# A graph-attention layer on one core: value products ahead of their softmax, and a tail with its own order

## The chip, the cores and the metric

The kernel runs on one core of one Trainium2 chip. The metric is device time in microseconds (us) of one execution. Three executions of the kernel before took 4083.7, 4086.26 and 4088.33 us; the median, 4086.26 us, is the time before.

## What is computed

A graph has 12500 nodes with 128 features each, and 400000 edges that are sorted by their target node. Each node's row goes through a layer norm and a ReLU to give h. Then, cut to what matters:

```
message = (h @ w_src + b_src)[src] + (h @ w_dst)[dst]
message = message * edge_weight * radial_mlp(edge_attr_32)
msg     = (message @ w_sep + b_sep).reshape(E, 8, 32)
alpha, value = smooth_leaky_relu(msg[:, :, :16]), msg[:, :, 16:]
score   = einsum('ehk,ahk->eh', alpha, alpha_dot)
att     = segment_softmax(score, dst)           # over the edges of a target
out     = segment_sum(value * att, dst) @ w_proj + b_proj
return x + out
```

So per edge there is a gathered row, a small perceptron of the edge's attributes, eight scores and a value row of 128; per target node there is a softmax over its edges and a weighted sum of values, which is projected and added to x.

## The kernel before

**Pairs, steps and lag.** Edges are cut into sections of 512 (four tiles of 128), and two sections make a pair; there are NP = 391 pairs, the last one short. A *half* is one section (c, f) of pair c. The loop calls `step(k)` for k = -5 to 390 and works on several pairs at once, in an order that is written out by hand: in step k it gathers the rows of pair k + 2, makes the message mT of pair k, the alphas of pair k - 1, and, for the pair c = k - LAG = k - 12, the weighted values and, one step later, the sums. The lag is there because the softmax runs over groups of MP = 8 pairs: eight pairs' scores are collected, then `softmax_up`, `softmax_down`, `softmax_sub` and `softmax_exp` scan them on DVE and ACT, and `softmax_T` turns the result into Pem, the attention factors by edge. Group 48, the last, has seven pairs, 384 to 390.

**The engines in a step.** POOL gathers each section by four indirect DMAs (L1018). PE turns the gathered rows and adds the targets' rows (L1078, L1090), multiplies for the perceptron (L1034, L1047, L1062), for the alphas (pa, L1101), the scores (L1118), the values (V, L1233) and the sums (L1246). V is one PSUM bank: `values(c, f)` multiplies mT of the half by w_v into it, and DVE multiplies V by Pem into pvx (L1235). `sums` multiplies pvx by a one-hot matrix oh of 64 targets (L1217, L1220) and DVE moves the sum with an addition to a tile ob (L1250). DVE also makes rad, mT and al (L1067, L1095, L1108), ACT the activations (sl is L1103). An engine takes its instructions in the order written, so an instruction that waits holds up those behind it.

**Where the sums go.** SP stores ob to two tables: whole windows of 64 targets to win (`store_win`), and rows of targets that lie inside one section to agg (`store`, two a pair, each after a value load of the row's place). Targets whose edges cross a section's end are combined from win later: `block_rows`, `block_columns`, `block_totals`, `block_quotients` and `rows_end`, for 13 blocks of 128 section ends; the last two blocks, 11 and 12, belong to the tail. Their rows are written to out by `scatter` (POOL, L1445).

**Units.** A unit is 512 rows of agg. `load_unit` and `load_x` bring its sums (gu) and its rows of x (xs); two steps later it has been divided by the softmax sums, turned, multiplied by w_proj, added to x and stored to out (L1303, L1308, L1312 to L1320, L1326, L1334, L1340, L1341). UNIT_STEP lists the steps at which the 23 units begin: before, the last ones are 366, 376, 386, 390 and 394.

**Direct pairs.** The last DIRECT = 13 pairs, 378 to 390, end too late for agg. For them `direct_quotients` divides the sums at once (L1264 to L1267), `direct_turn` and `direct_out` turn and project them and add the rows of x (L1272 to L1280), and `direct_scatter` writes them to out by target (POOL, L1287). Every such scatter and those of the blocks come after the last unit's store to out in the order of writes.

**The tail before.** After the loop POOL gathers 13 times rows of x by target for the direct pairs (L1460), loads the finished block rows, adds the output bias to the x rows (L1648) and gathers 13 times x for the blocks (L1454). Then `step(k)` is called 13 times more, for k = 391 to 403, with other conditions in it for k >= NP, and a list `jobs` puts the last blocks between the steps. The twelve pairs 379 to 390 get their V, their one-hots and their sums there. `sum_rows` (POOL, L1658) adds x to the block rows.

Of the kernel before, what the change touches and what calls it, by code (L numbers as in the profile page):

```python
# [55 lines left out]
def gnn_kernel(ctx: ExitStack, tc: tile.TileContext, a: dict, out: bass.AP):  # L56
# [19 lines left out]
    xb = dram.tile([N, C], F32, name="xb")  # L76
    win = dram.tile([NS * W, ROW], F32, name="win")
# [19 lines left out]
    assert D < IN_AGG and done(UNIT_STEP[-1]) < NS and UNITS * UNIT + P * 4 >= N - UNIT  # L97
    NF = N // P
# [82 lines left out]
    with tc.tile_pool(name="node", bufs=2) as np_, tc.tile_pool(name="node1", bufs=1) as n1, \  # L181
# [223 lines left out]
        def fits():  # L405
# [35 lines left out]
            nc.sync.dma_start(out=t_dst[N:N + W, :], in_=bare[:W, 0:C])  # L441
            nc.sync.dma_start(out=eb.rearrange("p s i -> p (s i)"),
# [470 lines left out]
    def windows():  # L913
# [7 lines left out]
        with tc.tile_pool(name="ps", bufs=1, space=PSUM) as pp, \  # L921
# [176 lines left out]
            def alphas(k, f):  # L1098
                pa = pp.tile([C, SEC], F32, name="pa")
# [124 lines left out]

            def values(c, f):
                if c >= NP - LAG and f == 0:
                    V = pms[:, c % 2, :].rearrange("p (t c) -> p t c", c=C)
                else:
                    V = pv
                n = tiles(c, f)  # L1230
                for t in range(n):
                    o = f * SEC + t * T
                    nc.tensor.matmul(V[:, t, :], mTs[c][:, o:o + T], w_v, start=True, stop=True)  # L1233
# [26 lines left out]

            def direct_quotients(c):
                o = accs[c]
                rd = sp.tile([P, H], F32, name="dr")
                nc.vector.tensor_scalar(rd, o[:, C:ROW], 1e-16, None, op0=ALU.add)  # L1264
# [3 lines left out]
                                     o[:, 0:C].rearrange("p (h k) -> p h k", h=H),  # L1268
                                     rd.unsqueeze(2).to_broadcast([P, H, C // H]))

            def direct_turn(c):
                nc.tensor.transpose(p3[:, 0, 0:P], dqs.pop(c), ident)  # L1272
                qTs[c] = sp.tile([P, C], F32, name="dT")
                nc.scalar.copy(qTs[c], p3[:, 0, 0:P])

            def direct_out(c):
                py = p3[:, 1, 0:C]
# [27 lines left out]
            def load_x(u, pool):  # L1305
                n0, n1, n = unit_rows(u)
                xs[u] = pool.tile([P, 4, C], F32, name="xs", bufs=1)
                (nc.scalar if u == UNITS - 1 else nc.sync).dma_start(out=xs[u][:n], in_=x[n0:n1, :].rearrange("(p t) c -> p t c", t=4))  # L1308
# [150 lines left out]
            def rows_dx(c):  # L1459
                nc.gpsimd.indirect_dma_start(  # L1460
                    out=xw_at(c), out_offset=None, in_=x[:, :],
                    in_offset=bass.IndirectOffsetOnAxis(ap=ids_d[:, c - D:c - D + 1], axis=0),
                    bounds_check=N - 1, oob_is_err=False)
# [25 lines left out]

            def step(k):  # L1490
                c = k - LAG
                if has(c - 2) and k <= NP:
# [16 lines left out]
                if has(c - 2) and k <= NP and c - 2 < IN_AGG:  # L1509
# [5 lines left out]
                if k % 16 == 7 and has(k + 9):  # L1515
                    prep_make((k + 9) // 16)
                unit = k >= UNIT_STEP[0]
# [10 lines left out]
                if k >= NP:  # L1528
                    m, r = LAST_M + 1, k - NP
                if has(c):  # L1530
                    weights(c)
                    values(c, 0)
# [8 lines left out]
                if c - 2 >= D and has(c - 2):  # L1541
                    direct_turn(c - 2)
# [11 lines left out]
                if has(k):  # L1554
                    mlp3(k)
                if has(k + 1):
# [6 lines left out]
                if has(c - 1):  # L1563
                    sums(c - 1)
                    if k >= NP:
                        if k == NP + LAG:
                            last_rows_2()
                        else:
                            store_win(c - 1)
# [279 lines left out]
```

## Time and profile before

| | before |
|---|---|
| time, median of 3 executions | 4086.26 us |
| the profiled execution's own time | 4089.07 us |
| its span, first to last instruction | 4087.2 us |
| PE busy | 3865.2 us (95%) |
| DVE busy | 3104.5 us (76%) |
| POOL busy | 3065.6 us (75%) |
| ACT busy | 1862.3 us (46%) |
| granted TensorE clock, mean | 0.985 |

The profiled execution is one more than the three, and a little longer than their median. Times within it count from the span's start. "Busy" leaves out what an engine spends on issuing, so an engine that issues DMAs back to back is not at 100%. In the rows of groups, the columns are line, engine, operation, output <- inputs with shapes, count, then busy us, mean ns of one, and the idle time ahead of them with what ended it; in rows of the timeline, the first two numbers are start and duration in us.

### The profile page before, as it was taken

The page shows a single profiled execution, that of the slowest core. Times are in us where ns is not written, and L with a number is a line of the kernel's source. Part 1 is how long each engine was busy: PE and PEld are TensorE (multiplying, and loading weights), DVE is VectorE, ACT ScalarE, POOL GpSimd, SP SyncE. Part 2 cuts the span into 40 slices and gives each one's busy share as a digit, 9 for nine tenths or more (in the row PEclk, how much of TensorE's full clock was granted, in tenths as well). Part 3 has the DMA queues.
Part 4 walks back from the last instruction along what each step waited for, and adds up shares of the span by engine and source line. Part 5 has one row for each costly group of instructions (what it writes and reads, how often), then busy time and mean ns, then how long its engine had stood idle before and what let it go on. Part 6 is the DMA issues. An engine that isn't in the chain of part 4 may idle for free.

```text
span 4087.2 us, 84249 instructions
## 1 busy us (share of the span) xinstructions
PE 3865.2 (95%) x27811; PEld 2349.3 (57%) x27811; DVE 3104.5 (76%) x5557; ACT 1862.3 (46%) x3782; POOL 3065.6 (75%) x3244
## 2 busy tenths in 40 slices
PE   7899999999999999999999999999999999999997
PEld 6356555655555555555555555555555556556555
DVE  6677777777777777777777777777777777777777
ACT  5454444444444444444444444444444444444451
POOL 6777777777777777777777777777777777777775
PEclk9999999999999999999999999999999999999998
DMA  7777777677767777777777777777777777777772
GB/s 242 214 186 194 182 193 193 184 182 190 191 169 195 186 191 172 196 187 180 185 192 185 190 189 197 194 174 192 197 194 183 185 191 198 182 195 193 186 177 55
DMA packets 536579, 762.21 MB, mean 186 GB/s; under 512 B 126743, under 2 KB 339769, under 8 KB 536006
## 3 DMA queue, kind: packets, MB, share of 16 engines
q1 hardware_dynamic: 378142, 498.27, 41.8%
q0 software_dynamic: 101872, 207.34, 24.5%
q10 hardware_dynamic: 56120, 51.10, 4.5%
q8 instruction: 226, 3.70, 0.4%
q14 instruction: 219, 1.79, 0.2%
HBM read 632.27 MB, written 125.70 MB: 185 GB/s over the span
## 4 chain that ended last, share of the span: by engine, by line
PE 68%; DMA 12%; POOL 7%; issue 5%; DVE 5%; ACT 2%; SPq 1%; ACTq 0%; DVEq 0%; POOLq 0%
PE V L1233 15%; PE pa L1101 14%; DMA gs<-t_src,idx 8%; PE misc L1246 8%; PE pm L1078 7%; PE p L1062 6%; POOL gs L1018 6%; PE m L1034 5%; PE pm L1090 4%; PE p L1047 4%; PE m L1118 3%; DMA agg<-ob 1%; DVE mT L1095 1%; POOL mT L1018 1%; DMA win<-ob 1%
## 5 line engine op out<-in xcount | busy, mean ns | idle before, releaser
L1018 POOL DMA_INDIRECT gs<-t_src,idx x3021 | 2875.4, 952 | 923.0 <-issue 768.5
L1103 ACT ACTIVATE sl<-pa,c_b_a 128x512 f32<-128x512 f32 x782 | 537.6, 687 | 1089.2 <-PE pa L1101 1085.1
L1108 DVE SCALAR_TENSOR_TENSOR al<-pa,sl 128x512 f32<-128x512 f32 x782 | 536.8, 686 | 527.6 <-ACT sl L1103 520.5
L1233 PEld LDWEIGHTS V<-c_w_v,mT 128*128 128x128 f32 x6154 | 753.3, 193 | 309.9 <-DVE ob L1250 119.9
L1233 PE MATMUL V<-c_w_v,mT 128*128 128x128 f32 x6154 | 886.3, 287 | 8.1 <-DVE pvx L1235 8.1
L1101 PE MATMUL pa<-mT,c_w_a 128*128 128x512 f32 x1564 | 839.2, 619 | 26.6 <-DVE mT L1095 23.5
L1235 DVE TENSOR_TENSOR pvx<-V,Pem 128x512 f32<-128x512 f32 x770 | 528.4, 686 | 207.9 <-PE V L1233 191.1
L1049 ACT ACTIVATE h<-p,b 128x512 f32<-128x512 f32 x391 | 469.2, 1200 | 427.5 <-PE p L1047 328.4
L1078 PEld LDWEIGHTS pm<-ident,gs 128*128 128x128 f32 x3021 | 375.2, 141 | 481.9 <-issue 463.8
L1067 DVE SCALAR_TENSOR_TENSOR rad<-p,c_fc_b,w_b 128x1024 f32<-128x1024 f32 x391 | 500.5, 1280 | 105.6 <-PE p L1062 87.3
L1246 PEld LDWEIGHTS misc<-pvx,oh 128*64 128x64 f32 x6250 | 353.1, 138 | 295.0 <-ACT h L1037 284.5
L1078 PE MATMUL pm<-ident,gs 128*128 128x128 f32 x3021 | 458.6, 275 | 64.5 <-DMA gs<-t_src,idx 64.4
L1095 DVE SCALAR_TENSOR_TENSOR mT<-pm,c_b_src,rad 128x1024 f32<-128x1024 f32 x391 | 497.6, 1273 | 7.7 <-PE pm L1090 7.2
L1246 PE MATMUL misc<-pvx,oh 128*64 128x136 f32 x6250 | 453.2, 287 | 0.9 <-ACT h L1037 0.3
L1062 PE MATMUL p<-h,w3b 64*128 64x512 f32 x1564 | 405.9, 596 | 0.5 <-ACT h L1049 0.4
L1034 PE MATMUL m<-eT,w1b 64*128 64x256 f32 x782 | 276.7, 434 | 20.3 <-ACT qT L1328 15.1
L1090 PE MATMUL pm<-ohT,m 64*128 64x512 f32 x1564 | 287.3, 445 | 0.0
L1101 PEld LDWEIGHTS pa<-mT,c_w_a 128*128 128x128 f32 x1564 | 237.3, 192 | 76.8 <-DVE mT L1095 44.5
L1034 PE MATMUL misc<-eT,w1b 64*128 64x256 f32 x782 | 276.8, 434 | 0.0
L1037 ACT ACTIVATE h<-misc,b 128x256 f32<-128x256 f32 x391 | 185.4, 474 | 193.9 <-PE misc L1034 181.1
L1134 ACT ACTIVATE Sp<-m,b_s 128x512 f32<-128x512 f32 x192 | 131.8, 686 | 308.5 <-PE m L1118 302.0
L1217 DVE TENSOR_TENSOR oh<-lane,misc 128x504 f32<-128x504 f32 x391 | 261.2, 668 | 0.1
(216 smaller groups left out, 3550.8 us busy)
## 6 DMA issues: line engine op xcount, KB each, us to landing
w_b<-in_edge_weight SPq DMA_DIRECT2D x390, 512.0 KB
d_b<-in_dst SPq DMA_DIRECT2D x390, 256.0 KB
e_t<-in_edge_attr ACTq DMA_DIRECT2D x386, 128.0 KB
sc_d<-Sp SPq DMA_DIRECT2D x192, 256.0 KB
gs<-t_src,idx POOLq DMA_INDIRECT x3021
win<-ob SPq DMA_DIRECT2D x390, 68.0 KB
agg<-ob SPq DMA_DIRECT2D x762, 33.5 KB
md<-t_dst SPq DMA_DIRECT2D x782, 32.0 KB
```

What stands on the lines that cost most here:

```text
L1018: sent = [nc.gpsimd.indirect_dma_start(out=gs[:, t, :], out_offset=None, in_=t_src[:, :], in_offset=bass.IndirectOffsetOnAxis(ap=idx[:, t0 ...
L1034: nc.tensor.matmul(p1[f], w1b[s, :], eTs[k][s, :], start=True, stop=True)
L1062: nc.tensor.matmul(p3[:, f, 0:SEC], w3b[s, :], h2s[k][s, :], start=True, stop=True)
L1067: nc.vector.scalar_tensor_tensor(rad[:, 0:n], p3.rearrange("c f e -> c (f e)")[:, 0:n], b3, w_g[k][:, 0:n], op0=ALU.add, op1=ALU.mult)
L1078: turned = [nc.tensor.matmul(pm[:, t * T:(t + 1) * T], gs[:, t, :], ident, start=(t == 0), stop=False, is_transpose=True, skip_group_check ...
L1095: nc.vector.scalar_tensor_tensor(mTs[k][:, 0:n], pms.rearrange("c f e -> c (f e)")[:, 0:n], b_n, rad[:, 0:n], op0=ALU.add, op1=ALU.mult)
L1101: nc.tensor.matmul(pa[:, 0:n], w_a, mTs[k][:, f * SEC:f * SEC + n], start=True, stop=True)
L1103: nc.scalar.activation(sl[:, 0:n], pa[:, 0:n], AF.Silu, bias=b_a, scale=1.0)
L1108: nc.vector.scalar_tensor_tensor(al, pa, 0.25, sl, op0=ALU.mult, op1=ALU.add)
L1233: nc.tensor.matmul(V[:, t, :], mTs[c][:, o:o + T], w_v, start=True, stop=True)
L1235: nc.vector.tensor_mul(pvx[c][:, f, 0:n, 0:C].rearrange("p t (h k) -> p t h k", h=H), V[:, 0:n, :].rearrange("p t (h k) -> p t h k", h=H), ...
L1246: nc.tensor.matmul(acc[f * W:(f + 1) * W, :], ohs[c][:, f * TS + t, :], pvx[c][:, f, t, :], start=(t == 0), stop=(t == n - 1), skip_group_ ...
```

## The change

It has four parts.

1. **Value products ahead.** `values` is split. `product_v` makes V; `values_ahead` does that for a half whose softmax may not be there yet, and ACT copies V back over the half's own mT. `values` then multiplies by Pem from that copy. `plan(k)` hands out the halves in order, two a step as before and three at steps 311, 315, ... 387, at three spots of the step. After the loop four halves are left: those of pairs 389 and 390.
2. **Units.** The late units begin at 376, 381, 387 and 393 in place of 376, 386, 390 and 394: one more is done within the loop.
3. **Rows of x.** A table xp in memory holds the last 2048 rows of x with the output bias added; it is made in steps 40 to 47 (`padded_rows`). SP loads each direct pair's two windows of 64 consecutive rows from it, in the last three steps of the loop and one in the tail (`rows_dx`). POOL's 13 gathers and its additions go. The last unit's x comes from xp as well.
4. **A tail of its own.** The extra 13 calls of `step` are replaced by a list written out, with `slot(c)` as its repeated part. The sums of a direct pair start from a product of the identity with the matrix bare, stay in PSUM for the quotients, and are copied to ob by ACT; they stand ahead of the turning of an older pair. The rows of x are added by PE (identity times the rows, into the same sum) and ACT copies the result. The softmax of group 48 stands ahead of the slots 380 to 390. The block rows come back by SP, and so do the last rows of block 12 (`last_rows_2`).

The diff, cut to its core:

```diff
-UNIT_RUNS = ((96, 32, 4), (204, 13, 7), (296, 10, 10), (390, 4, 2))
+UNIT_RUNS = ((96, 32, 4), (204, 13, 7), (296, 10, 9), (381, 6, 3))
+EXTRA = 311
...
+            def values_ahead(c, f, V):
+                n = tiles(c, f)
+                product_v(c, f, V)
+                nc.scalar.copy(value_slot(c, f)[:, 0:n, :], V[:, 0:n, :])
+                ahead.add((c, f))
...
             def values(c, f):
+                n = tiles(c, f)
+                if (c, f) in ahead:
+                    V = value_slot(c, f)
                 else:
                     V = pv
+                    product_v(c, f, V)
...
+            def direct_start(c):
+                accs[c] = half[:, 0:ROW] if c == D else pms[:, c % 2, 0:ROW]
+                nc.tensor.matmul(accs[c], ident, bare, start=True, stop=False, skip_group_check=True)
+            def direct_sums(c):
+                acc = accs[c]
...
+                            nc.tensor.matmul(acc[f * W:(f + 1) * W, :], ohs[c][:, f * TS + t, :],
+                                             pvx[c][:, f, t, :], start=False, stop=(t == n - 1),
+                                             skip_group_check=True)
+            def direct_rows(c):
+                accs[c], acc = sp.tile([P, ROW], F32, name="ob", bufs=5), accs[c]
+                nc.scalar.copy(accs[c], acc)
+                if c == NP - 1:
+                    last_rows_2()
+                else:
+                    store_win(c)
+                if c < IN_AGG:
+                    store(c, 0)
+                    store(c, 1)
...
             def direct_out(c):
-                nc.tensor.matmul(py, qTs.pop(c), w_proj, start=True, stop=True)
-                y = xw_at(c)
-                nc.vector.tensor_add(y, py, y)
+                nc.tensor.matmul(py, qTs.pop(c), w_proj, start=True, stop=False)
+                nc.tensor.matmul(py, ident, xw_at(c), start=False, stop=True)
+                nc.scalar.copy(xw_at(c), py)
...
             def rows_dx(c):
-                nc.gpsimd.indirect_dma_start(
-                    out=xw_at(c), out_offset=None, in_=x[:, :],
+                at = [nc.sync.value_load(base[0:1, f, c:c + 1]) for f in range(2)]
+                for f in range(2):
+                    nc.sync.dma_start(out=xw_at(c)[f * W:(f + 1) * W, :], in_=xp[ds(at[f], W), :])
...
+            def plan(k):
+                c = k - LAG
+                n = 3 if k >= EXTRA and (k - EXTRA) % 4 == 0 else 2
+                todo = [next(halves) for _ in range(n)] if has(c) else []
+                at = [todo[0:1], todo[1:-1], todo[-1:]]
...
+            def slot(c):
+                if has(c):
+                    weights(c)
+                    for f in range(2):
+                        values(c, f)
+                if D < c <= NP:
+                    direct_sums(c - 1)
+                    direct_quotients(c - 1)
+                    direct_rows(c - 1)
+                if has(c - 2):
+                    direct_turn(c - 2)
+                if has(c):
+                    one_hot(c)
+                    direct_start(c)
+                if has(c - 2):
+                    direct_out(c - 2)
```

The tail's order, with LM = 48, u = 22 and c0 = 380: stores of pair 377; `block_rows_back`; sums of 378; `scores(389)`; value products of 389; alphas of 390; the values of 379; `scores(391)`; quotients and rows of 378; `softmax_up`; one-hot of 379; value products of 390 beside `softmax_down`; `softmax_sub` with its stores of the maxima; `softmax_exp`; `load_x(22)`; slot 380; `load_unit(22)`; `rows_dx(390)`; `block_load(12)`; slot 381; `softmax_T`; slot 382; the unit's quotients and turning; `block_maxima(12)`; slot 383; the unit's products and its store to out; `sum_rows` and the scatters of blocks 0 to 10, then the direct scatters that are ready; `block_factors(12)`; slots 384 to 392 with the rest of block 11 between them; the last rows; block 12.

More of the change, by code (lines that the diff above doesn't have):

```diff
@@ L1508, in step @@
                     load_sm(k // MP)
-                if has(c - 2) and k <= NP and c - 2 < IN_AGG:
+                if has(c - 2) and c - 2 < IN_AGG:
                     store(c - 2, 1)
@@ new lines, in windows @@
+            unit_turn(u, sp, m1)
+            block_maxima(last)
+            slot(c0 + 3)
+            unit_product(u, m1)
+            unit_out(u)
+            sum_rows()
+            for g in range(last - 1):
+                scatter(g)
+            late_out.append(u)
+            direct_scatter()
+            block_factors(last)
+            block_exp(last)
+            slot(c0 + 4)
+            block_rows(last - 1)
+            slot(c0 + 5)
+            slot(c0 + 6)
+            block_columns(last - 1)
```

203 lines of the change are left out of this document (124 added, 79 removed).

## The prediction, made before the changed kernel was run

> **What bounds the kernel now.** I read three stretches separately: steps 311 to 390 of the loop (the change adds work there), the moment the loop ends, and the tail. First, busy time by stretch: the last 830 us of the loop, and what follows.
>
> ```profile
> 3170.00:4000.00 830.00, 797.81 (x5785) 485.43 (x5781) 642.14 (x1128) 376.15 (x759) 629.16 (x661) 0.99 0.72 187
> 4000.00:4087.20 87.20, 60.45 (x482) 47.53 (x482) 62.09 (x163) 12.76 (x50) 47.59 (x48) 0.86 0.19 50
> ```
>
> Columns are the length, then PE, PEld, DVE, ACT, POOL busy, the granted clock, DMA share, GB/s. In the loop PE is busy 797.81 of 830 us. POOL looks less loaded, but its group of gathers says otherwise:
>
> ```profile
> L1018 POOL DMA_INDIRECT gs<-t_src,idx x645 | 613.7, 951 | 196.6 <-issue 163.6 <-DMA gs<-t_src,idx 9.8 <-PE V L1233 4.6
> ```
>
> 645 gathers of 0.951 us with 0.305 us between them fill 810 us: POOL never stops, and eight gathers a step are 10.0 us. So two engines could pace the loop. The chain of waits in an ordinary stretch decides between them:
>
> ```profile
> 3603.62 1.09 PE V L1233 x8
> 3604.71 0.86 PE pa L1101 x2
> ...
> 3612.40 1.09 PE V L1233 x8
> ...
> 3622.17 1.09 PE V L1233 x8
> ```
>
> V to V is 8.78 us in one step, 9.77 us in the next (which has the scores), and all of the chain between is PE. Those steps are shorter than 10.0 us; softmax steps, units and stalls bring the mean to it. Then I ask how long a gathered section lies ready before PE turns it, in mid-loop and for the last section:
>
> ```profile
> 1671.29 0.94 POOL L1018 DMA_INDIRECT gs<-t_src,idx  x1 [0.30 <-issue]
> ...
> 1675.81 0.60 PE L1078 MATMUL pm<-ident,gs 128*128 128x128 f32 x4
> ```
> ```profile
> 3981.30 0.94 POOL L1018 DMA_INDIRECT gs<-t_src,idx  x1 [0.30 <-PE m L1334]
> ```
> ```profile
> 3998.02 0.27 PE L1078 MATMUL pm<-ident,gs 128*128 128x128 f32 x1
> ```
>
> (Each POOL row is the last gather of its section.) In mid-loop PE turns the rows 3.6 us after the gather: there POOL paces. At the end they lie for 15.8 us: **PE paces the last 80 steps**, and what is added to it there is paid.
>
> The tail runs from the last message (3999.55 + 0.88 = 4000.43) to 4087.2: 86.8 us.
>
> ```profile
> 3999.55 0.88 DVE L1095 SCALAR_TENSOR_TENSOR mT<-pm,c_b_src,rad 128x640 f32<-128x640 f32 x1
> ```
> ```profile
> 4043.16 0.34 SPq L1341 DMA_DIRECT2D out<-xs  x1
> ```
> ```profile
> 4046.14 1.03 POOL L1287 DMA_INDIRECT out<-gs,ids_d  x1 [23.75 <-DVE dq L1267]
> ...
> 4054.91 3.47 POOL L1658 TENSOR_TENSOR w_b<-w_b,gs 128x512 f32<-128x512 f32 x3
> ...
> 4081.73 0.91 POOL L1445 DMA_INDIRECT out<-w_b,ids  x1 [0.30 <-issue]
> ```
>
> POOL sits idle 23.75 us, starts scattering 3.0 us after unit 22's rows leave for out (4043.16; the rows of that store must be overwritten, so this releases it, not the dq named, long done), and then never stops until 4082.64: 26 scatters and the 3.47 us of sums. The end follows 4.56 us behind. So **unit 22's store sets the end**: whatever brings it earlier brings the end earlier, as long as DVE's last blocks keep up. They were ready at 4079.98, 1.75 us before the last scatter's issue:
>
> ```profile
> 4079.70 0.28 DVE L1676 TENSOR_TENSOR w_b<-w_b,gs 28x128 f32<-28x128 f32 x1
> ```
>
> **The change, part by part.** *Loop.* The loop did 758 halves' V products; it now does 778, twenty more (steps 311, 315, ... 387). Each is the 1.09 us row: 20 x 1.09 = **21.8 us** later. Their new ACT copies (0.59 us each by the unit's copy row below, two a step) come ahead of sl in ACT's queue; PE's pa runs 0.86 us beside each, so sl starts no later; ACT is busy 376 of 830 us. If that cover failed, 0.6 us a step, some 45 us; I take nothing. The multiply pvx no longer waits for V, which frees DVE, not PE.
>
> One more unit lies wholly in the loop (381 and 387 in place of 386; the unit of 390 was finished in the tail):
>
> ```profile
> 3673.80 0.45 PE m L1326 x4
> ...
> 3674.27 0.59 ACT qT L1328
> ```
> ```profile
> DVE xs L1312 <- DMA xs<-in_x: 9.3, 3, 5.4
> ```
>
> Turning 0.45, PE waiting for the copy 0.59, products as V's 1.09: **2.1 us**. Waits for x are 9.3 us over nine units, so one unit more costs **1.0 us** (bounds 0 and 5.4).
>
> The padded rows (four loads, DVE adds of 0.68, stores) come in steps 40 to 47, far within the stretch that POOL paces: nothing; uncovered, 2.7 us. SP's 26 loads with 26 register reads stand in the last three steps, when the loads of coming steps have run out: nothing; what is late then is needed only at the direct products. POOL loses 13 gathers and four adds, about 21 us, but sat idle 23.75 us afterwards: nothing by itself. *End of loop: 21.8 + 2.1 + 1.0 = 24.9 us later.*
>
> *Tail.* V is gone from it but for four halves; the sum's eviction moves to ACT, the residual add to PE. What sets the end is unit 22, so I follow its chain. DVE's rows in the tail:
>
> ```profile
> L1235 DVE TENSOR_TENSOR pvx<-pm,Pem 128x512 f32<-128x512 f32 x12 | 8.2, 682 | 2.9 <-PE pm L1233 2.9
> L1217 DVE TENSOR_TENSOR oh<-lane,misc 128x504 f32<-128x504 f32 x12 | 8.0, 671 | 0.0
> ...
> L1267 DVE TENSOR_TENSOR dq<-ob,dr 128x128 f32<-128x128 f32 x13 | 4.0, 306 | 0.4
> ...
> L1265 DVE RECIPROCAL dr<-dr 128x8 f32<-128x8 f32 x13 | 2.6, 203 | 0.4
> L1264 DVE TENSOR_SCALAR dr<-ob 128x8 f32<-128x8 f32 x13 | 2.5, 193 | 0.4
> L1220 DVE TENSOR_TENSOR oh<-misc,far 128x8 f32<-128x8 f32 x12 | 2.0, 163 | 0.0
> ...
> L1155 DVE TENSOR_TENSOR_SCAN M<-m,S 128x512 f32<-128x512 f32 x1 | 1.2, 1210 | 0.0
> L1160 DVE TENSOR_TENSOR_SCAN M<-m,M 128x512 f32<-128x512 f32 x1 | 1.2, 1209 | 0.0
> L1131 DVE TENSOR_TENSOR S<-m,S 32x512 f32<-32x512 f32 (+1 forms) x2 | 1.0, 482 | 1.4 <-PE m L1118 1.4
> L1108 DVE SCALAR_TENSOR_TENSOR al<-pa,sl 128x512 f32<-128x512 f32 (+1 forms) x2 | 1.0, 476 | 0.0
> ...
> L1169 DVE TENSOR_TENSOR M<-S,M 128x512 f32<-128x512 f32 x1 | 0.7, 694 | 0.0
> ```
>
> Ahead of the stores of the maxima: two pvx 1.36, one score add as L1169 0.69, al 0.95, score adds 0.96, quotients 0.70, scans 2.42, one-hot 0.83, L1169 0.69 and a copy, 0.2: 8.8 us. PE has sums, scores and a V product ahead of the last alphas, and DVE waits for sl and for scores: I add 2.3 (0 if all overlaps, 5 if nothing does): **11.1 us** after the loop. Then SP's queue:
>
> ```profile
> 4018.45 1.68 DMA agg<-ob
> ...
> 4020.26 1.37 DMA agg<-ob
> ```
> ```profile
> 4017.34 0.35 SPq L1254 DMA_DIRECT2D win<-ob  x1
> ...
> 4027.25 3.35 SPq L1182 DMA_DIRECT2D max_d<-both  x5
> ...
> 4031.04 0.37 SPq L1303 DMA_DIRECT2D gu<-agg  x1
> ```
> ```profile
> 3661.71 3.96 DMA xs<-in_x
> ```
>
> The maxima hold SP 3.8 us (4027.25 to 4031.04). Pair 379's window row and its two agg stores now stand *behind* them, with the load of x: 0.4 + 4.3 (4017.34 to 4021.63). Then gu's load, 4.0 by the nearest row, of x: **12.5 us**. DVE meanwhile does slots 380 to 382 and then waits some 4 us. Quotients and maxima about 1.9 (an estimate: 0.69 as L1320 below, and eight small ops), slot 383 2.9, the last add 0.7, landing 3.0: **8.5 us**. One term comes from PE's idling while DVE waits:
>
> ```profile
> 3669.10 2.08 PE V L1233 x8
> ```
>
> That V, after a 4 us gap, took 2.08 us for 1.09. At that rate unit 22's turning and products take 1.3 us more: **1.3**. First scatter: 11.1 + 12.5 + 8.5 + 1.3 = 33.4 us after the loop (45.7 before). Then 26 scatters, 36.5 - 3.5 = 33.0, the sums now done while POOL waits, and 4.6: **71.0 us**, against 86.8: 15.8 saved. DVE's own path: seven slots at 2 x 0.682 + 0.671 + 0.306 + 0.203 + 0.193 + 0.163 = 2.9 us behind the unit's add at 30.4, and about 12 for the two blocks and the last rows (an estimate: some 4 each, and the last sums): about 63 us, 2 before POOL's last issue. Without that cover, its excess is paid.
>
> [...]
>
> ```profile
> 4000.34 3.33 DVE L1393 TENSOR_TENSOR de<-up,cuts 128x128 f32<-128x128 f32 x1
> ```
> ```profile
> L1320 DVE TENSOR_TENSOR gu<-gu,ru x23: 691/691/694, 1040.5 to 4035.6; 128x512 f32<-128x512 f32 x23
> ```
>
> L1393, both inputs in SBUF, took 3.33 us while POOL added rows; L1320, of pvx's size and inputs in SBUF, took 691 to 694 ns beside POOL's gathers. So only POOL's 3.5 us of sums can hold pvx, in a stretch where DVE waits anyway: nothing. [...]
>
> **Sum.** +24.9 - 15.8 = +9.1 us. The profiled execution took 4089.07 us (span 4087.2 and 1.87 around it), so 4098.2 against itself; it lies 2.8 above the median of the runs, 4086.26, so **4095** as a median.
>
> **Rivals.** *A. The added products are hidden* because POOL's 10.0 us a step still paces. It decides where rows wait 4 us or less, as in mid-loop; 15.8 us speaks against it. The loop ends 3.1 later: +3.1 - 15.8, 4074 us, faster. *B. Half clock through the whole tail*: with V gone PE rests between slots. Prelude PE work of 4 us doubles (+4), each of seven slots grows from 2.9 to 3.9 (sums 1.08 to 2.16): DVE's 63 becomes 74, past POOL, and the end 79.6: 4104 us, slower. It decides when the clock falls in each slot; 0.86 granted in a tail with PE busy 60 of 87 us speaks half for it. [...] *C. Unit 22 is early and part of the loop's idle 32 us swallows products*: gu 2 us sooner, all waits overlapping, loop +22: end 68.6 at best by DVE's path: +22 - 18.2, 4090 us, no change. *D. SP's rows come too late* for the direct products: needs 10 us of delay; in B.
>
> **How the numbers follow.** 0.2% (8.2 us) is about what a measurement can tell here: 4078 to 4094 is no change. Forecast 0.58, its own range 4088 to 4102, of it 0.22 up to 4094 and 0.36 above; A 0.12; B 0.15; C 0.15. Faster 0.12, same 0.22 + 0.15 = 0.37, slower 0.36 + 0.15 = 0.51. Range 4084 to 4105: it leaves out A and a part of B.
>
> **What would show it.** Right: V to V steps unchanged but 1.09 longer at every fourth from 311; last gather still near 3982, last message near 4025, its section lying about 40 us; no POOL adds beside the prelude; the first scatter some 33 us behind the last message, then no POOL gap. Wrong: a last message before 4015 (A), slots of 4 us at clock 0.5 (B), POOL gaps behind its first scatter, or new PE waits on ACT's copies.

## The result, and the profile after

The changed kernel takes 4106.23 us (median of 4100.37 to 4113.22), the kernel before 4086.2 in the same set of runs: ratio **1.0049, 95% interval 1.0036 to 1.0062**, slower by 20 us. The prediction was 4095, and its range ended at 4105. The profiled execution is the shortest of its set, 4100.37 us (span 4098.5); that of before took 4089.07. So the two traces differ by 11.3 us, and the medians by 20; what follows divides the 11.3. The other 8.7 us, by which the medians lie further apart than these two executions, stand in no trace.

Busy time by stretch, of before and then of the changed kernel: from the message of step 310 to that of step 390, and from the end of the last message to the end.

```profile
3195.90:3999.60 803.70, 773.06 (x5605) 469.68 (x5597) 622.01 (x1092) 367.10 (x740) 608.96 (x641) 0.99 0.72 187
4000.40:4087.20 86.80, 60.45 (x482) 47.53 (x482) 61.69 (x163) 12.76 (x50) 47.19 (x47) 0.86 0.19 51
```
```profile
3193.40:4011.90 818.50, 789.81 (x5783) 485.74 (x5777) 616.44 (x1097) 461.49 (x915) 624.38 (x638) 1.00 0.70 184
4012.80:4098.50 85.70, 54.78 (x345) 40.53 (x344) 45.89 (x130) 19.33 (x79) 32.31 (x32) 0.70 0.18 51
```

The loop's last stretch is 14.8 us longer, of which PE is busy 16.75 more; step 310 came 2.5 us sooner, for a reason that I did not trace; the tail is 1.1 us shorter, where 15.8 was forecast. PE is busy 5.7 us less there, at a lower granted clock (0.70 for 0.86).

**The loop** does what was said. The messages of steps 334 to 336, of before and of the changed kernel; step 335 has a third half:

```profile
3435.95 1.28 DVE L1095 SCALAR_TENSOR_TENSOR mT<-pm,c_b_src,rad 128x1024 f32<-128x1024 f32 x1
3445.73 1.27 DVE L1095 SCALAR_TENSOR_TENSOR mT<-pm,c_b_src,rad 128x1024 f32<-128x1024 f32 x1
3454.50 1.27 DVE L1095 SCALAR_TENSOR_TENSOR mT<-pm,c_b_src,rad 128x1024 f32<-128x1024 f32 x1
```
```profile
3436.01 1.27 DVE L1101 SCALAR_TENSOR_TENSOR mT<-pm,c_b_src,rad 128x1024 f32<-128x1024 f32 x1
3446.87 1.27 DVE L1101 SCALAR_TENSOR_TENSOR mT<-pm,c_b_src,rad 128x1024 f32<-128x1024 f32 x1
3455.65 1.27 DVE L1101 SCALAR_TENSOR_TENSOR mT<-pm,c_b_src,rad 128x1024 f32<-128x1024 f32 x1
```

9.78 us became 10.86, and the next step is 8.77 or 8.78 in both: 1.08 or 1.09 us, paid in full. Over all twenty such steps it is 21.7 us.

**The tail's chain**, SP's queue first (start, length, line; x8 is eight loads), then DVE and POOL:

```profile
4005.43 7.02 SPq L1518 DMA_DIRECT2D gs<-xp  x8
4017.44 7.01 SPq L1518 DMA_DIRECT2D gs<-xp  x8
...
4033.21 3.39 SPq L1188 DMA_DIRECT2D max_d<-both  x5
...
4042.21 0.37 SPq L1349 DMA_DIRECT2D gu<-agg  x1
```
```profile
4027.19 0.16 DVE L1183 COPY both<-M 128x2 f32<-128x2 f32 x1
...
4044.99 0.18 DVE L1373 TENSOR_SCALAR ru<-gu 128x32 f32<-128x32 f32 x1 [4.64 <-DMA gu<-agg]
```
```profile
4056.36 1.41 POOL L1501 DMA_INDIRECT out<-w_b,ids  x1 [20.11 <-DMA out<-xs]
```
```profile
4092.68 0.92 POOL L1501 DMA_INDIRECT out<-w_b,ids  x1 [2.41 <-DVE w_b L1733]
```

The loop ends at 4012.8, but SP is at its third group of row loads until 4024.45. Then come its stores for pairs 377 and 378 and two block loads, and only at 4033.21 the maxima, which were ready at 4027.35. The first scatter starts 43.6 us behind the loop's end (33.4 forecast, 45.7 before), and the last one waits for DVE. In the slots PE waits for a copy:

```profile
PE pm L1283 <- ACT ob L1307: 12.3, 11, 2.1
...
PE p L1324 <- ACT dT L1320: 1.5, 2, 1.1
```

(Total, times, longest.) A slot's first product (L1283) waits in eleven slots, 12.3 us in all, for ACT's eviction of the slot before, though that lies in the other half of pm.

### The profile page after: what moved, and what is told of

Read it like the earlier page. It is cut to its first block, busy times and chain, and to the rows that moved or that the text cites. A ratio compares the mean times of both kernels' runs of the same rounds, so it can differ in the third digit from the quotient of the medians.

```text
span 4098.5 us, 84668 instructions
## 1 busy us (share of the span) xinstructions
PE 3874.3 (95%) x27863; PEld 2357.5 (58%) x27863; DVE 3081.3 (75%) x5534; ACT 1962.9 (48%) x3986; POOL 3064.9 (75%) x3225
## 5 line engine op out<-in xcount | busy, mean ns | idle before, releaser
L1234 PE MATMUL V<-c_w_v,mT 128*128 128x128 f32 x6234 | 895.6, 287 | 1.5 <-DVE pvx L1255 1.4
L1255 DVE TENSOR_TENSOR pvx<-V,Pem 128x512 f32<-128x512 f32 x604 | 414.8, 687 | 167.0 <-PE V L1234 151.5
L1266 PEld LDWEIGHTS misc<-pvx,oh 128*64 128x64 f32 x6048 | 340.8, 137 | 279.4 <-ACT h L1043 271.7
L1101 DVE SCALAR_TENSOR_TENSOR mT<-pm,c_b_src,rad 128x1024 f32<-128x1024 f32 x391 | 497.5, 1272 | 4.8 <-PE pm L1096 4.5
L1266 PE MATMUL misc<-pvx,oh 128*64 128x136 f32 x6048 | 437.5, 287 | 1.5 <-ACT h L1043 1.4
```

Source lines behind the costliest of these rows:

```text
L1101: nc.vector.scalar_tensor_tensor(mTs[k][:, 0:n], pms.rearrange("c f e -> c (f e)")[:, 0:n], b_n, rad[:, 0:n], op0=ALU.add, op1=ALU.mult)
L1255: nc.vector.tensor_mul(pvx[c][:, f, 0:n, 0:C].rearrange("p t (h k) -> p t h k", h=H), V[:, 0:n, :].rearrange("p t (h k) -> p t h k", h=H), ...
L1266: nc.tensor.matmul(acc[f * W:(f + 1) * W, :], ohs[c][:, f * TS + t, :], pvx[c][:, f, t, :], start=(t == 0), stop=(t == n - 1), skip_group_ ...
```

## The experiments

Theory: the tail's gain went to SP's row loads, which hold the maxima and by them unit 22, and to slots made serial by the eviction; the loop pays its products. Rivals: half the clock alone makes the slots long; the products in the loop cost little and the tail's new order loses; the copies and the reading of V from SBUF cost.

All but one of these runs came to chips on which the kernel before takes about 5300 us and single executions of one kernel lie up to 75 us apart. The mean granted clock is 0.91 to 0.93 there (0.985 on the first), and PE stands idle for reasons that the trace does not name. Total times say little there. So I compare two stages, steps 310 to 390 and the tail (from the end of the last message), among chips of that kind, with the kernel before and the changed one run there too.

**Both kernels on such chips.**

> The kernel before itself, for the stages that the variants are compared with on a chip of 5300 us. Theory: its loop from step 310 to 390 takes what the variant without products ahead took (1015 to 1020 us), 10 to 40 less than those with them; its tail 100 to 104 us, within 3 us of the changed kernel's 101.3. Rival (the changed tail does gain and the loop loses more): tail over 108 us.

> The changed kernel itself, so that its stages can be compared with those of the variants on one and the same chip. Theory: loop from step 310 to 390 longer than the variants without products ahead by 20 to 30 us where the chip takes 5300 us (15 to 20 where it takes 4090); tail 6 to 8 us longer than with POOL's rows and two tiles. Rival (the variants' own edits did nothing, and chips differ): loop and tail as in the variants, within 2 us.

Stretches as above, before and then changed:

```profile
4178.60:5200.50 1021.90, 834.39 (x5592) 495.60 (x5591) 617.47 (x1092) 359.83 (x740) 598.46 (x628) 0.94 0.56 146
5201.40:5302.10 100.70, 68.77 (x482) 55.04 (x482) 57.26 (x162) 12.94 (x50) 32.34 (x33) 0.77 0.12 33
```
```profile
4162.90:5190.90 1028.00, 846.19 (x5771) 509.83 (x5771) 618.16 (x1096) 448.62 (x915) 591.98 (x613) 0.96 0.55 145
5191.80:5293.10 101.30, 54.33 (x346) 40.27 (x344) 46.06 (x130) 19.36 (x79) 30.73 (x29) 0.68 0.15 42
```

The tails are 100.7 and 101.3: here too the change gains nothing. In time the changed kernel stands at 1.0036 (0.9999 to 1.0072) of before.

But the two tails are not alike. Behind its first scatter the changed kernel's has a stretch of 10.9 us in which PE, DVE and ACT all do nothing, though the sums that DVE is to read next are done at its start; "remote" says that the trace names nothing in the program that ended the wait:

```profile
5249.95 2.08 PE L1291 MATMUL pm<-pvx,oh 128*64 128x136 f32 x16
...
5263.38 0.17 DVE L1298 TENSOR_SCALAR dr<-pm 128x8 f32<-128x8 f32 x1 [11.23 <-remote]
```

I call this a stall. Every tail of the new order on these chips has one behind the first scatter, 6.1 to 14.1 us long; those of the old order have none over 2.7 us, and neither order has one on a chip of the quick kind (4086 us). What makes it is not known. So tails on these chips compare the stalls as well, and what lies ahead of the first scatter is the safer measure.

**Rows by POOL.** SP's row loads are undone:

```diff
-                at = [nc.sync.value_load(base[0:1, f, c:c + 1]) for f in range(2)]
-                for f in range(2):
-                    nc.sync.dma_start(out=xw_at(c)[f * W:(f + 1) * W, :], in_=xp[ds(at[f], W), :])
+                nc.gpsimd.indirect_dma_start(
+                    out=xw_at(c), out_offset=None, in_=x[:, :],
+                    in_offset=bass.IndirectOffsetOnAxis(ap=ids_d[:, c - D:c - D + 1], axis=0),
+                    bounds_check=N - 1, oob_is_err=False)
```

All 13 stand behind the loop, ahead of `rows_x`, and POOL adds b_out to them, as before.

> The changed kernel with the direct products' x rows gathered by POOL behind the loop as before the change, and the bias added by POOL; SP loads no rows. Theory (SP's 26 loads keep the maxima's store, and by it gu's load and unit 22, late): maxima stored some 14 us behind the loop's end, first scatter 39 to 41 us behind it in place of 43.6: 4099 to 4104, 3 to 6 us faster than the changed kernel. Rival (SP's queue costs nothing, or POOL's 13 gathers come to be late themselves): 4105 or more, and the first scatter still over 43 us behind the loop's end.

> The changed kernel with the direct products' x rows gathered by POOL behind the loop, looked at once more for its tail. Theory (SP's 26 loads hold the maxima's store, gu's load and by them unit 22): maxima stored 14 us behind the loop's end in place of 20.4, first scatter 39 to 41 us behind it in place of 43.6, tail 81 to 84 us in place of 85.7. Rival (the slots' length alone sets the tail): first scatter at 43 us or later, tail 85 or more.

The chain of the changed kernel and of the second of these runs; their loops end at 5191.8 and 5222.5:

```profile
5203.93 0.17 DVE L1183 COPY both<-M 128x2 f32<-128x2 f32 x1
5212.06 3.39 SPq L1188 DMA_DIRECT2D max_d<-both  x5
5221.51 0.37 SPq L1349 DMA_DIRECT2D gu<-agg  x1
5237.20 1.41 POOL L1501 DMA_INDIRECT out<-w_b,ids  x1 [21.84 <-DMA out<-xs]
```
```profile
5236.14 0.17 DVE L1183 COPY both<-M 128x2 f32<-128x2 f32 x1
5236.33 3.34 SPq L1188 DMA_DIRECT2D max_d<-both  x5
5244.84 0.38 SPq L1349 DMA_DIRECT2D gu<-agg  x1
5262.06 1.52 POOL L1501 DMA_INDIRECT out<-w_b,ids  x1 [31.61 <-issue]
```

With SP's loads the maxima wait 8.0 us for the queue (5203.93 + 0.17 to 5212.06), without them 0.02. gu's load comes 22.3 us behind the loop's end for 29.7, the first scatter 39.6 for 45.4 (39.0 in the first run). The tails are 95.9 and 97.1 for 101.3. The theory holds: some 6 us up to the first scatter, 4 to 5 in the tail. The total, 1.0034 (1.0007 to 1.0061), doesn't show it: that interval is 29 us wide.

**Two tiles.** The accumulators alternate between two tiles:

```diff
-                accs[c] = half[:, 0:ROW] if c == D else pms[:, c % 2, 0:ROW]
+                accs[c] = half[:, 0:ROW] if c == D else (pv.rearrange("p t c -> p (t c)") if c % 2 else pms[:, 0, :])[:, 0:ROW]
```

> The changed kernel with the direct accumulators taken in turn from the V tile and from the first half of pm, in place of the two halves of pm, so that a slot's first product can't wait for the eviction of the slot before. Theory (that wait of 0.8 to 2.1 us in each of eleven slots makes the slots serial): slots 3.6 us in place of 4.4, first scatter 2 us sooner and no gaps of POOL behind it, 3 to 8 us faster than the changed kernel. Rival (slots are paced by TensorE at half clock or by DVE): the wait goes and another takes its place, within 1.5 us of the changed kernel.

> The changed kernel with its direct accumulators alternating between two tiles, once more. Theory: slots of 3.3 to 3.8 us, first scatter 1 to 3 us sooner, no gap of POOL behind it: 4099 to 4104. Rival: another wait takes the place of the one removed, 4105 to 4108.

> The changed kernel with the direct accumulators alternating between two tiles, looked at once more for its tail. Theory (the wait of a slot's first product for the eviction of the slot before makes the slots serial): first scatter 41 to 42.5 us behind the loop's end in place of 43.6, slots 3.3 to 3.9 us, tail 82 to 84.5 us in place of 85.7. Rival (half clock or SP's queue alone sets the tail): first scatter at 43 us or later, tail 85 or more.

Tails 98.1, 94.8, 98.0 for 101.3; first scatters 45.5, 43.5, 43.2 for 45.4. The wait of L1283 is gone, and PE waits for the copy dT instead (L1324: 16.8 us in ten waits in the first of these runs, 8.3 in the second), as the rival had it. The tails are 3 to 6 us shorter, but without the stalls behind the first scatter they take 85.7, 88.2 and 85.1 for 88.4, and the run `early` below, whose tail is the changed kernel's own, 91.1. A gain is not shown. Totals 1.0027 (1.0005 to 1.0049) and 1.0028 (1.0005 to 1.0052).

**Both edits.**

> The changed kernel with two parts of its tail undone: the direct products' x rows are gathered by POOL behind the loop, with POOL's adds of the bias, as in the kernel before, so that SP has no rows to load; and the direct accumulators alternate between the V tile and the first half of pm, so that no slot's first product waits for the eviction of the slot before. Theory: the maxima are stored right after they are ready, some 15 us behind the loop's end in place of 20; gu's load goes 4 to 6 us earlier; the first scatter comes 36 to 39 us behind the loop's end in place of 43.6, and the tail is 77 to 81 us in place of 85.7. Rival (half the clock sets the tail): first scatter no earlier than 42 us behind the loop, tail 84 or more.

> The changed kernel with POOL's rows and two tiles, timed. Theory (the loop's 15 to 20 us stay, the tail is 7 to 8 us shorter than before's): ratio to before 1.001 to 1.003 on a chip of 4086 us, between the changed kernel (1.0049) and before. Rival (the first look at 4089 was a chance of the loop's stalls): 1.004 or more on such a chip. On a chip of 5300 us: tail 90 to 94 us against 101 of the changed kernel there, and a ratio of 1.002 to 1.004.

The first of these ran on a chip of the quick kind: 4088.77 us, beside 4084.9 of before. Its stretches, its chain (loop's end 4008.1), and PE's longest wait in the slots:

```profile
3187.30:4007.20 819.90, 791.07 (x5783) 485.57 (x5777) 616.55 (x1097) 461.28 (x915) 625.44 (x639) 1.00 0.71 184
4008.10:4086.90 78.80, 50.18 (x344) 36.80 (x344) 46.19 (x130) 19.33 (x79) 50.36 (x49) 0.78 0.20 52
```
```profile
4021.87 0.16 DVE L1183 COPY both<-M 128x2 f32<-128x2 f32 x1
4022.06 3.35 SPq L1188 DMA_DIRECT2D max_d<-both  x5
4031.44 0.38 SPq L1349 DMA_DIRECT2D gu<-agg  x1
4045.30 1.04 POOL L1501 DMA_INDIRECT out<-w_b,ids  x1 [1.40 <-issue]
```
```profile
PE p L1324 <- ACT dT L1320: 14.9, 13, 3.3
```

Tail 78.8 us: 6.9 under the changed kernel's, 8.0 under before's. First scatter 37.2 us behind the loop for 43.6: 6.4 of the 6.9 us lie ahead of it, where the maxima now leave 0.03 us after they are ready for 5.9, so the two tiles are left with some 0.5 us. The wait that two tiles took from L1283 (12.3 us) stands now at L1324, for dT: 1.5 us became 14.9. ACT copies dT behind ob, and ob starts only when DVE's dq has ended (0.08 us behind it in twelve of the thirteen slots), though the sums were done 0.8 us or more before. So the serial chain is sums, DVE, ob, dT, next sums; copying ob ahead of the quotients was not tried. On the 5300 us chips the tail is 91.3 for 101.3, and the total 1.0032 (1.0014 to 1.0050). The loop's 15 to 16 us are still there. So this too is slower than before, by the interval on the 5300 us chips; the one execution of each on the quick chip, 3.9 us apart, can't tell.

**Half the clock.** Six idle products in each slot, whose results nothing uses:

```diff
+                    for _ in range(WARM):
+                        nc.tensor.matmul(pv[:, 0, :], ident, ident, start=True, stop=True)
                     direct_start(c)
```

> The changed kernel with six more products of 128 columns (of a constant, into the V bank that is free by then, used by nothing) in each slot of the tail, just ahead of the slot's first product, where TensorE otherwise waits for the eviction. They add 0.8 us of work at full clock and give nothing to the output. Theory (half clock doubles the sums, 2.08 us for 1.15, because TensorE rests in each slot): granted clock over 0.9 in the slots, sums 1.15 us throughout, slots 3.3 to 3.9 us, tail 2 to 6 us shorter than the changed kernel's on the same chip. Rival (the serial wait for the eviction is the length of a slot, and the clock only follows it): the clock rises, the slots stay within 0.3 us, the tail within 1.5 us or longer.

From 14 to 50 us behind the loop, changed kernel and keep_warm:

```profile
5205.80:5241.80 36.00, 23.24 (x134) 18.33 (x135) 17.78 (x50) 7.20 (x34) 8.10 (x7) 0.56 0.24 66
```
```profile
5220.60:5256.60 36.00, 27.39 (x240) 23.97 (x237) 20.60 (x55) 8.39 (x40) 8.27 (x7) 0.85 0.25 69
```

The clock rose from 0.56 to 0.85, and the tail stayed: 101.5 for 101.3, first scatter 44.6 for 45.4. That decides less than I hoped. The six products took 1.5 us where PE ran at full speed, and not the 0.8 that I had expected, and the stalls behind the first scatter are 15.7 us in this tail for 12.9. A gain of some us may be hidden behind both. What the traces do show is that sums at a low clock take longer: in the changed kernel's tail on the first chip eight of the twelve groups of sums (L1291) took 1.91 to 2.08 us at a granted clock of 0.50 to 0.57, and the others 1.14 or 1.15 at 1.00, which is 0.8 to 0.9 us of a slot. Whether the tail's end would come sooner without it stays open. Total 1.0024 (0.9999 to 1.0048).

**The products, alone and without.** loop_part is before's code, its tail included, with `plan`, `values_ahead` and the first line below; no_ahead is the changed kernel with the other edit.

```diff
+                n = 3 if k >= EXTRA and (k - EXTRA) % 4 == 0 else 2
```
```diff
-EXTRA = 311
+EXTRA = 10**6
```

> The kernel before with the loop's part of the change alone: from step 311 on, every fourth step multiplies a third half's V ahead and copies it to mT's place, and the kernel before's own tail uses what is then ready. Theory (the added V products are paid in full, and the gain they should bring in the tail is small): the loop ends some 20 us later (20 halves of 1.09 us, a little of it taken up by stalls), the tail is a few us shorter, so 12 to 20 us slower than before: 4098 to 4106. Rival (the loop's part costs little, and the changed tail's order loses the time): 4080 to 4090.

> The kernel before with the loop's part of the change alone, and its own tail, once more. Theory: the loop ends 15 to 22 us later, and the old tail, which POOL and SP set, gains less than 6 us by the V's that it loses: 4096 to 4107. Rival (the V's in the loop are hidden or their gain comes back in the tail): 4080 to 4090.

> The changed kernel without the products ahead: no third half in any loop step, and each slot of the tail multiplies its own V's, which pvx reads from PSUM. Theory: the loop ends within 4 us of the kernel before; the tail gets 20 halves back, but TensorE then holds its full clock and its sums cost 1.15 us for 2.08, so slots grow from 4.4 to no more than 5.5 us: 4084 to 4094, that is 12 to 20 us faster than the changed kernel. Rival (slots are slow for TensorE's work, and V in them adds 2.2 us to each of eleven): 4105 or more, no faster than the changed kernel.

> The changed kernel without the products ahead once more, since the first runs of it came out too far apart to tell. Theory: the loop ends within 4 us of the kernel before, the slots take no more than 5.5 us each: 4084 to 4094, 12 to 20 us faster than the changed kernel (4106). Rival (slots are slow for TensorE's work, and the V's in them are paid as in the loop): 4102 or more.

> The changed kernel without the products ahead, a third time, since the chip of the first two took 5300 us for the kernel before and its runs lay 60 us apart. Theory: the loop ends within 4 us of the kernel before; slots of the tail, each with its own V's at full clock, take no more than 5.5 us: ratio to before 0.9995 to 1.002 (4084 to 4094). Rival (slots are slow for TensorE's work, and the V's in them are paid as in the loop): 1.004 or more (4102).

One profile of each (loop, tail), loop_part_2 and no_ahead_2:

```profile
4182.40:5242.90 1060.50, 863.80 (x5749) 519.34 (x5749) 620.30 (x1091) 450.48 (x914) 616.21 (x632) 0.94 0.54 141
5243.80:5337.70 93.90, 52.15 (x322) 36.67 (x322) 56.89 (x163) 13.00 (x50) 29.57 (x29) 0.68 0.12 34
```
```profile
4185.10:5200.80 1015.70, 834.87 (x5611) 497.21 (x5611) 619.15 (x1096) 360.24 (x738) 585.96 (x613) 0.95 0.56 146
5201.70:5320.10 118.40, 70.71 (x506) 56.76 (x504) 46.68 (x130) 19.36 (x79) 29.13 (x29) 0.84 0.13 37
```

Loop: without products ahead 1020.3, 1015.7, 1020.0 and before's 1021.9; with them in these steps 1025.2 to 1054.0 in the eight profiles of the changed kernel and its tail variants (mean 1040.6, 21 more), 1058.8 and 1060.5 in loop_part. On the mean they are paid. But single profiles say little here: loop_part's two are 37 and 39 us over before's, where twenty halves of 1.09 us make 21.8, and early_pool_tiles (below), which has no third half in these steps, took 1033.1. Tail: the old order without those V's takes 95.3 and 93.9, 5 to 7 us less than with them; the new order with them takes 118.0, 118.4 and 120.3, 17 to 19 more than without. My expectation for no_ahead fell: in the new order slots of 7 us came out, and the total can't be told from the changed kernel's, 1.0030, 1.0031 and 1.0030 (the widest 1.0006 to 1.0056). loop_part gave 1.0028 (1.0003 to 1.0053) and 1.0049 (1.0026 to 1.0072). So on these chips, V's gone, the old order has the shorter tail: 94 to 95 against 101.3. The stall of 10.9 us, which the old order has not, is more than that difference, and loop_part was not run on a quick chip. Whether the new order itself loses is not shown.

**Copies.** Before, with every loop half's V copied by ACT and read from SBUF:

```diff
+                if c < NP - LAG:
+                    V, pV = mTs[c][:, f * SEC:(f + 1) * SEC].rearrange("p (t c) -> p t c", c=C), V
+                    nc.scalar.copy(V[:, 0:n, :], pV[:, 0:n, :])
```

> The kernel before, with nothing moved: in every loop step ScalarE copies each half's V to mT's place, and pvx reads it from SBUF in place of PSUM. Theory (a pvx with two SBUF inputs holds a gather that starts beside it, 0.3 to 0.45 us each, about one gather in ten): over the 290 steps that POOL paces 0.2 to 0.3 us a step are paid, 50 to 90 us slower than before, with many gathers over 1.15 us in the whole loop. Rival (the copies and the reading from SBUF cost nothing; the long gathers of the changed kernel come of its other parts): 4086 within 5 us.

1.0091 (1.0067 to 1.0116): 48 us slower, near what was expected, but not by the path that was expected. Gathers over 1.15 us were 100 of 2320 up to step 310 (16 in before_again), yet POOL is some 60 us ahead of PE on these chips and can't be what is paid. PE's products pa waited longer for the message. PE's own idle time ahead of L1101 from 1000 to 4000 us, before_again and copy_alone:

```profile
  DVE mT L1095: 45.3, 47
```
```profile
  DVE mT L1095: 130.6, 106
```

DVE's multiply stands behind a copy, and the message behind the multiply. But other waits shrank, and PE's idle time as a whole did not rise: 552 us in that stretch, and 542 with the copies. PE did 1% fewer products there and was busy 11 us longer at them, at a granted clock of 0.92 for 0.94. So what is paid stays open. In the changed kernel's loop on the first chip PE's waits for the message are 8.1 us for before's 3.8.

**Earlier products.** The twenty halves at steps 231 to 307, alone and with both edits of the tail:

```diff
-EXTRA = 311
+EXTRA = 231
...
-                n = 3 if k >= EXTRA and (k - EXTRA) % 4 == 0 else 2
+                n = 3 if k in range(EXTRA, EXTRA + 80, 4) else 2
```

> The changed kernel with its twenty halves ahead at steps 231 to 307, where POOL paces the loop, in place of 311 to 387. Theory (a product ahead is paid where TensorE paces and is hidden where POOL paces; what remains is the gathers held by pvx reading SBUF, now in 160 steps): on a chip of 4086 us the loop ends 4 to 12 us later than before in place of 15 to 20, so 4090 to 4101; on a chip of 5300 us, where POOL waits for TensorE all along, as late as the changed kernel within 6 us. Rival (the products cost the same wherever they stand): the changed kernel's time within 3 us on either.

> The changed kernel with three edits: POOL gathers the direct products' x rows, the accumulators alternate between two tiles, and the twenty halves ahead stand at steps 231 to 307 in place of 311 to 387. Theory (a product ahead is hidden where POOL paces; the first two edits give the tail 78 to 80 us on a chip of 4086 us): the loop ends 4 to 12 us later than before, the tail is 7 to 8 us shorter: ratio to before 0.999 to 1.001 on such a chip. Rival (products cost the same wherever they stand): loop 15 to 20 us later, ratio 1.002 to 1.003. On a chip of 5300 us, where POOL waits for TensorE in the whole loop, both say 1.002 to 1.004.

1.0041 (1.0015 to 1.0067) and 1.0040 (1.0022 to 1.0059). The message of step 310 stood at 4220.0 and 4213.9 us (4178.6 in before_again), the steps behind it took 1018.7 and 1033.1, and the tails 103.3 and 93.1. Both theories allow this where POOL never paces; whether products are hidden where it does stays open.

## Why the prediction was wrong

In the two profiled executions the loop came out 12.6 us better than forecast and the tail 14.7 us worse. That their sum, +11.3 us, lies so near the forecast +9.1 is luck.

1. *Loop, +24.9.* Measured +12.3 at the last message (+14.8 in the stretch, +16.1 in pool_and_tiles). The products cost what was said: PE paces, and over the twenty steps with a third half the time from message to message is 21.7 us longer. What was not forecast: four other steps, 317, 341, 357 and 373, took 13.5, 13.6, 15.3 and 17.0 us before and 11.0, 11.2, 11.7 and 11.5 after, 14.0 us less; the remaining 56 came out 7.1 longer. (In pool_and_tiles: 24.2 longer, 12.9 less, 4.9 longer.) In those four steps of before a load had come late. DVE waited for rows of x, pvx stood behind that, and PE's next V behind pvx; or ACT waited for a load, its copy rx stood behind that, and PE behind rx. PE's waits in this stretch of before, and DVE's for x after the change (before it, 9.3 us in three):

```profile
PE V L1233 <- DVE pvx L1235: 7.0, 2, 4.4
PE misc L1409 <- ACT rx L1405: 6.9, 2, 5.0
```
```profile
DVE xs L1368 <- DMA xs<-in_x: 3.8, 3, 1.8
```

After the change no V waits for pvx, and the waits for rx are 2.6 us. Behind the old waits PE also ran below full speed: the granted clock of these four steps read 0.80 to 0.97 before and 1.00 after. So "frees DVE, not PE" was wrong, and one unit more did not cost 1.0 us of waiting for x. New are 5.0 us of waits for gathers and 4.3 more for the message. Why the loads came sooner I did not trace.
2. *The step that failed*: "SP's 26 loads with 26 register reads stand in the last three steps ... nothing; what is late then is needed only at the direct products". What was late was SP itself. A group of eight loads and reads holds its queue 7.0 us, the third group lay behind the loop's end, and the maxima stood behind it: 5.9 us in this profile. Without SP's row loads the first scatter came 5.8 and 6.4 us sooner behind the loop on the 5300 us chips (rows_by_pool) and 6.4 on the quick one (pool_and_tiles).
3. *11.1 to the maxima*: 14.4 (4027.19 - 4012.8), as DVE waited 3.42 us for PE, whose V's took 2.07 us, at a granted clock of 0.50; the one V of 2.08 us in the prediction had the same clock. I had given that rate to unit 22's products alone.

```profile
4019.92 2.07 PE L1234 MATMUL pm<-c_w_v,mT 128*128 128x128 f32 x8
```
```profile
4025.32 1.22 DVE L1166 TENSOR_TENSOR_SCAN M<-m,M 128x512 f32<-128x512 f32 x1 [3.42 <-PE m L1156]
```

4. *SP chain 12.5, then 8.5 + 1.3*: 11.8 (4033.21 to 4044.99) and 11.4 (4044.99 to 4056.36): near. With 14.4 and 5.9 it makes 43.5, the measured 43.6.
5. *33.0 and 4.6*: 37.2 (4056.36 to 4093.60, the end of the last scatter) and 4.9. "About 63 us, 2 before POOL's last issue" fell: slots took 3.3 to 5.2 us and not 2.9, so POOL had gaps and the last scatter waited 2.41 for DVE. My 2.9 added DVE's instructions. It left out that ob waits for dq and the next product for ob, and that the sums of eight of the twelve groups run at a granted clock of 0.50 to 0.57, in 1.91 to 2.08 us. The tail's miss of 14.7 us is then SP's queue 5.9, the maxima 3.3, SP's chain -0.7 and 1.6 (point 4), and 4.2 and 0.3 behind the first scatter: 14.6.
6. *pvx from SBUF.* I held that it costs nothing, since L1320 took 691 to 694 ns beside gathers and only L1393 was long beside POOL's adds (3.33 us; the median of its 13 is 0.285). I looked at the wrong engine: it is the gather that is held. A pvx, a gather that started in it, and all gathers from 3170 to 4000 us:

```profile
3816.99 0.69 DVE L1255 TENSOR_TENSOR pvx<-mT,Pem 128x512 f32<-128x512 f32 x1 [0.33 <-ACT Pem L1207]
```
```profile
3817.26 1.23 POOL L1024 DMA_INDIRECT gs<-t_src,idx  x1 [0.30 <-issue]
```
```profile
L1024 POOL DMA_INDIRECT gs<-t_src,idx x646 | 632.7, 979 | 196.9 <-issue 161.2 <-DMA gs<-t_src,idx 9.7 <-PE V L1234 5.5
```

The mean gather went from 0.951 to 0.979 us, 18 us over 646 (0.028 each). The 87 gathers that start inside a multiply from two SBUF inputs take 1.141 us on the mean, the 539 others of the stretch from step 310 on 0.955. The last message now comes 13.4 us behind the last gather's end, 17.3 before. The multiplies are not held by gathers: the 118 that start inside a gather take 0.679 us on the mean, the 36 others 0.685. PE paid little: its waits for gathers in the stretch are 5.0 us in five, for none before.
7. *Rivals.* A (products hidden) fell by the loop. B (half the clock) came out nearest in time, at 4104, and its half clock is in the trace, in the V's of point 3 (0.50) and in eight of the twelve groups of sums (0.50 to 0.57), with waits of PE for ob of 2.1 us at most; but it didn't know of SP's queue, and what the clock alone costs is open (keep_warm). C had the loop right, whose idle time swallowed a part of the products, and the tail wrong, where unit 22 was not early. D (SP's rows too late for the direct products) had the right engine and the wrong victim.

No version that I ran beat the kernel before. The tail was mended (78.8 us for 86.8, in one execution), the loop's products were not.

## What to carry to other kernels

Work that is moved to an idle queue is free only if nothing urgent is queued behind it: follow each queue to the first later instruction on the critical chain, here five small stores behind a group of eight loads and what had queued up after it (5.9 us). For a repeated slot add up the chain through all engines, evictions and shared accumulator tiles included, and not the busiest engine's instructions, at the clock that the trace shows there (0.70 in this tail, 0.56 in 36 us of after_again's). A product moved from a stage where an engine waits to one that it paces was paid at once here (21.7 us for twenty), and must win more than that at the other end. Follow the idle times that the trace before shows as well: here four stalls behind late loads shrank and paid for more than half of it.

## What the runs showed of the hardware

- One program (before, before_again) took 4086 us on one chip and 5300 on others: granted clock 0.985 and 0.926, gathers 0.952 and 0.949 us, but PE, DVE and POOL all less busy from 2000 to 3000 us. Of PE's 197 us of idle time there, 136 end with nothing that the trace names.

```profile
2000.00:3000.00 1000.00, 958.16 (x6947) 578.70 (x6944) 766.29 (x1340) 458.92 (x923) 757.88 (x795) 0.99 0.73 188
```
```profile
2000.00:3000.00 1000.00, 802.52 (x5316) 472.69 (x5314) 586.37 (x1040) 345.00 (x710) 583.29 (x614) 0.94 0.56 144
```

- In the changed kernel, a gather that starts while DVE multiplies from two SBUF inputs takes 1.14 us on the mean for 0.955, and 1.45 at most; the multiply is not held by a gather that started before it (0.679 and 0.685 us).
- In the changed kernel's slots ACT's copy of an accumulator starts only after DVE's last read of the same one (0.07 or 0.08 us behind it in twelve of thirteen), 0.8 us behind that engine's first (4073.87 and 4074.68).
- With fillers (keep_warm) the granted clock rose from 0.56 to 0.85 (PE busy 27.4 us of 36 for 23.2), and the tail, its stalls included, was no shorter (101.5 us for 101.3).
